# A four-layer gated transformer on one core: the head of layer 3's attention drawn into the 8-bit unit of layer 2, and gated adds moved from VectorE to ScalarE and GpSimd

## The chip, the cores and the metric

The kernel runs on one core of a Trainium2 chip. Its time is the device time of one execution in microseconds (us), of which the median over several runs is taken. The engines are TensorE (PE in the profile, with its weight loads as PEld), VectorE (DVE), ScalarE (ACT), GpSimd (POOL) and SyncE (SP, which issues transfers). The profile is one execution, recorded by the hardware.

## What is computed

The input x has 4 sequences of 256 tokens with 256 features. Four layers follow; each adds a cross attention and then a feed-forward unit, both on a layer norm of x and both gated:

```python
x = x + jnp.tanh(g_xattn[2]) * _L2_xattn_ref(_layernorm(x, axis=-1), ctx_512, ...)
x = x + jnp.tanh(g_ffn[2]) * _L2_ffn_ref(_layernorm(x, axis=-1), ...)
x = x + jnp.tanh(g_xattn[3]) * _L3_xattn_ref(_layernorm(x, axis=-1), ctx_512, ...)
x = x + jnp.tanh(g_ffn[3]) * _L3_ffn_ref(_layernorm(x, axis=-1), ...)
```

Layers 0 and 1 are of the same form with other units. What matters here are the units of layers 2 and 3. Their attention is plain: queries are x times a 256x256 matrix, keys and values come from a context of 64 positions, there are 16 heads of 16 features, the mask is causal, and the heads' outputs go through a 256x256 matrix. The feed-forward unit of layer 2 is a linear map in 8 bits: each row of the normalized x is scaled so that its largest magnitude is 127, rounded to whole numbers, multiplied with a weight rounded likewise, scaled back, and a bias is added. The feed-forward unit of layer 3 is a mixture of 8 experts, of which each token takes 2, and a shared expert.

## The kernel before

The 1024 tokens are 8 tiles of 128 tokens (tiles 0 to 7), and these make two groups of four (groups 0 and 1). x stays in SBUF for the whole kernel. The program is written with a tile framework: pools hand out buffers in turn, waits follow from who writes and reads a tile, and a scheduler of the framework, when the kernel is built, sets the order in which each engine's instructions stand in that engine's queue. So the order on an engine is not the order of the Python text. Each engine then works through its queue in order. `behind(later, sooner)` is the one means by which the text asks for an order within an engine.

**Attention of layers 2 and 3** (`attention23`, L1014). `queries(g)` makes the queries of one group: `layernorm` (L426: statistics on DVE L431 and L434, a square root on ACT L436, a reciprocal on DVE L439; then the normalization, on DVE L450 for layer 2, on ACT L447 for layer 3, where DVE first makes a shift, L443), `transposed` (PE L462, copies by ACT L169 and DVE L171), a product with the query weights (PE L477) and a scaling on ACT (L1034). Group 0's queries are made ahead of the loop over tiles, group 1's beside it.

`in_flight` (L514) runs the loop over tiles as a pipeline of depth three. In a step it makes the scores of one tile (PE L1058, causal mask L1048 for even tiles; maximum on DVE L1071, subtraction on DVE L1073, exponential on ACT L1082), weights the tile before (sum on DVE L491, reciprocal L492, product on POOL L493), attends with the tile before that (transposes on PE L507, two copies attnT on ACT L508, values on PE L1090, a copy ctxTok on ACT L1099, output weights on PE L1102), and adds the output of the oldest tile to x by `gated_add` (DVE L512, one instruction that reads the output from PSUM). ACT has one table of functions at a time; the square root and the exponential are in different ones, and each switch is an instruction ACT_TABLE_LOAD in its queue. Identity, copies and multiplications need no switch.

**The 8-bit unit** (`ffn2`, L1977). `rounded(g)` normalizes a group (L447), takes the largest magnitudes (DVE L1963), scales and rounds (DVE L1968, L1970), and adds the gated bias to x on POOL (L1974). `rounded(0)` is called near the end of layer 2's attention (`beside2`), `rounded(1)` when the loop of `ffn2` begins, since both groups stand in its list. For each group the loop then transposes (PE L1985, copy by ACT L1986), multiplies (PE L1991), scales (DVE L1995) and adds to x (POOL L1996).

**Buffers.** Transposed groups are in a pool xT of two buffers. Scores and their transposes (attn, attnT) take turns in a pool t4 of six buffers of 128x1024. Small row tiles (xn, y, ctxTok) take turns in a pool of seven.

## Time and profile before

| what | value |
|---|---|
| median of 3 runs | 839.23 us (837.9 to 839.84) |
| the profiled execution | 837.3 us, span 835.4 us |
| PE busy | 772.9 us, 93% of the span |
| DVE busy | 497.3 us, 60% |
| ACT busy | 291.6 us, 35% |
| POOL busy | 246.4 us, 29% |
| attention of layer 2 (first L477 to last L1102) | 539.76 to 592.25 us |
| attention of layer 3 (first L477 to last L1102) | 610.28 to 661.34 us |

The span runs from the first to the last instruction; the profiled execution's own time is longer by 1.9 us, for what lies around the span. A line of the timeline gives a start, a duration (of a merged run of instructions, where x4 or the like stands at its end), engine, line, operation, tiles and shapes; in brackets stand the idle time before it and what ended that. In the view by windows each row is a stretch of time with the busy time of each engine. The granted clock is the share of full speed that TensorE was given.

### The profile page before, as it was taken

What the parts mean: (1) busy time and instruction counts of PE and PEld (TensorE: products, weight loads), DVE (VectorE), ACT (ScalarE), POOL (GpSimd) and SP (SyncE); (2) the same over time, 40 slices, a digit from 0 to 9 for tenths busy, and PEclk for the clock granted to TensorE, in tenths of its full rate; (3) what the DMA queues carried; (4) which work ended last, traced back from release to release, by engine and by line L of the source; (5) the groups of instructions that cost most, each with busy time, mean ns of one, the idle gap of its engine ahead of it and who ended that gap; (6) DMA issues with size and microseconds to landing.
All of it is one profiled execution on the core that took longest, in us unless ns stands there. A gap on an engine that the chain in (4) does not pass through costs nothing.

```text
span 835.4 us, 12470 instructions
## 1 busy us (share of the span) xinstructions
PE 772.9 (93%) x4492; PEld 519.2 (62%) x4492; DVE 497.3 (60%) x1146; ACT 291.6 (35%) x508; POOL 246.4 (29%) x211
## 2 busy tenths in 40 slices
PE   6999999898999999999999989998579899999993
PEld 4544443687575776676555746655236557999993
DVE  5565454874682554545879559788869664334320
ACT  2121112343312333322633477166455521233320
POOL 1355454322132343321031200024424203344222
PEclk9999999999999999999999999899789999999997
DMA  9510215700121253324900001800000102222223
GB/s 343 189 39 0 62 40 204 262 22 4 29 72 40 72 141 83 74 35 123 378 17 7 1 1 37 324 24 1 26 0 2 51 8 78 55 51 46 33 26 71
DMA packets 32740, 64.14 MB, mean 77 GB/s; under 512 B 5121, under 2 KB 19713, under 8 KB 31905
## 3 DMA queue, kind: packets, MB, share of 16 engines
q1 hardware_dynamic: 25216, 52.56, 18.2%
q0 software_dynamic: 7104, 9.93, 7.3%
q8 instruction: 39, 0.64, 0.3%
q10 hardware_dynamic: 352, 0.79, 0.3%
q14 instruction: 29, 0.23, 0.1%
HBM read 53.86 MB, written 10.45 MB: 77 GB/s over the span
## 4 chain that ended last, share of the span: by engine, by line
PE 51%; DVE 9%; ACT 4%; issue 1%; POOL 1%; DMA 0%; POOLq 0%; DVEq 0%; ACTq 0%
PE wide L1435 9%; PE wide L477 7%; PE mm L1451 4%; PE mm L1525 3%; PE mm L709 3%; PE mm L1899 3%; PE mm L1883 2%; PE wide L961 2%; PE wide L1562 2%; PE wide L1563 2%; PE mm L1774 2%; PE mm L477 2%; DVE sm L491 1%; PE mm L507 1%; PE mm L1102 1%; PE wide L1058 1%
## 5 line engine op out<-in xcount | busy, mean ns | idle before, releaser
L493 POOL TENSOR_TENSOR attn<-attn,sm 128x1024 f32<-128x1024 f32 x32 | 61.1, 1913 | 229.3 <-DVE sm L492 179.0
L477 PE MATMUL wide<-xT,big 128*128 128x512 f32 (+1 forms) x240 | 108.6, 600 | 1.1 <-DVE shared L1656 0.9
L737 DVE TENSOR_TENSOR rope<-wide,big 128x512 f32<-128x512 f32 x96 | 59.6, 682 | 52.0 <-PE wide L477 52.0
L477 PEld LDWEIGHTS wide<-xT,big 128*128 128x128 f32 (+1 forms) x240 | 43.4, 188 | 57.3 <-issue 49.3
L1435 PE MATMUL wide<-blk,still 128*128 128x128 f32 x640 | 74.8, 275 | 0.6 <-DVE blk L1407 0.6
L1435 PEld LDWEIGHTS wide<-blk,still 128*128 128x128 f32 x640 | 73.1, 192 | 0.8 <-issue 0.8
L709 PE MATMUL mm<-vo,attnT 128*128 128x256 f32 x256 | 58.6, 382 | 1.5 <-ACT attnT L508 1.5
L477 PE MATMUL wide<-xT,dense 128*128 128x512 f32 (+1 forms) x120 | 55.1, 599 | 0.0
L709 PEld LDWEIGHTS mm<-vo,attnT 128*128 128x128 f32 x256 | 47.8, 190 | 11.4 <-ACT attnT L508 3.2
L508 ACT COPY attnT<-mm 128x512 f32<-128x512 f32 x64 | 34.4, 587 | 46.2 <-PE mm L507 45.7
L491 DVE TENSOR_REDUCE sm<-attn 128x16 f32<-128x1024 f32 x32 | 38.7, 1208 | 15.2 <-ACT attn L485 13.8
L1397 DVE COPY still<-big 128x1024 f32 x20 | 13.9, 693 | 52.0 <-PE wide L1435 44.5
L1466 POOL DMA_INDIRECT sums<-ring,scratch x20 | 31.6, 1578 | 40.4 <-ACT ring L1462 18.8
L1466 POOL DMA_INDIRECT sums<-ring,big x17 | 27.0, 1591 | 48.5 <-ACT ring L1545 18.2
L507 PE MATMUL mm<-ident,attn 128*128 128x128 f32 x256 | 33.7, 275 | 5.7 <-POOL attn L493 5.7
L1370 POOL DMA_INDIRECT xs<-xd,scratch x20 | 20.0, 1002 | 62.3 <-PE mm L1404 34.0
L512 DVE SCALAR_TENSOR_TENSOR x<-mm,tg,x 128x256 f32<-128x256 f32 x44 | 20.5, 471 | 29.4 <-PE mm L709 18.2
L1451 PE MATMUL mm<-big,hidden 128*128 x160 | 37.7, 379 | 0.0
L507 PEld LDWEIGHTS mm<-ident,attn 128*128 128x128 f32 x256 | 29.1, 141 | 13.3 <-POOL attn L493 8.5
L1443 ACT ACTIVATE hidden<-wide 128x512 f32<-128x512 f32 x20 | 12.0, 599 | 72.8 <-PE wide L1435 67.5
L477 PEld LDWEIGHTS wide<-xT,dense 128*128 128x128 f32 (+1 forms) x120 | 21.5, 185 | 24.4 <-issue 22.7
L791 ACT COPY big<-mm 128x512 f32<-128x512 f32 x16 | 8.6, 589 | 68.0 <-PE mm L779 61.7
(359 smaller groups left out, 1572.1 us busy)
## 6 DMA issues: line engine op xcount, KB each, us to landing
big<-in_L_w_gate_up SPq DMA_DIRECT2D x8, 1024.0 KB, 12.1
big<-in_L_w_down SPq DMA_DIRECT2D x8, 512.0 KB, 8.9
w_L_qk<-in_L_qk SPq DMA_DIRECT2D x4, 896.0 KB
big<-in_L_w SPq DMA_DIRECT2D x2, 1480.0 KB, 7.9
big<-in_L_w SPq DMA_DIRECT2D x2, 1110.0 KB
big<-in_L_wo SPq DMA_DIRECT2D x1, 2048.0 KB
big<-in_L_w SPq DMA_DIRECT2D x2, 1024.0 KB, 5.3
xd<-xn SPq DMA_DIRECT2D x16, 128.0 KB, 1.8
```

What stands on the lines that cost most here:

```text
L477: nc.tensor.matmul(ps, w(c), xT[:, c, :], start=(c == 0), stop=(c == 1))
L491: nc.vector.tensor_reduce(sm, e, AX.X, ALU.add)
L493: nc.gpsimd.tensor_tensor(e, e, sm.unsqueeze(2).to_broadcast([P, groups, n]), ALU.mult)
L507: nc.tensor.transpose(ps[:, i * P : (i + 1) * P], ev[:, pr * P : (pr + 1) * P], ident)
L508: nc.scalar.copy(aT[:, half * 4 : half * 4 + 4, :].rearrange("p i t -> p (i t)"), ps)
L709: nc.tensor.matmul(ps[:, :D], aT[:, s, :], vo[:, s, :], start=(s == 0), stop=(s == NP - 1))
L737: nc.vector.tensor_tensor(m[:, s, :].rearrange("q (b t) -> q b t", t=S), ps[:, s, :].rearrange("q (b t) -> q b t", t=S), table, ALU.mult,)
L1435: nc.tensor.matmul(ps[:, k, f : f + P], w[:, at : at + P], st[:, c * P : (c + 1) * P], start=(c == 0), stop=(c == 1),)
L1451: nc.tensor.matmul(ps[:, :D], hT[:, j * P : (j + 1) * P], self.w[:, bass.ds(r + j * D, D)], start=(j == 0), stop=(j == n - 1),)
L1466: nc.gpsimd.indirect_dma_start(out=self.sums[b % len(self.sums)], out_offset=bass.IndirectOffsetOnAxis(ap=self.scatter[:, b : b + 1].bitca ...
L1525: nc.tensor.matmul(ps[:n, f : f + P], w[:, c * FU0 + f : c * FU0 + f + n], st[:, c * P : (c + 1) * P], start=(c == 0), stop=(c == 1),)
L1899: nc.tensor.matmul(ps[:, :D], terms[:, k, f, i * P : (i + 1) * P], w2[:, f, :], start=(f == 0 and k == 0), stop=(f == 7 and k == 2),)
```

## The change

There are four parts.

- `layernorm` can load a table behind its square root. Group 1's norm in the attention of layers 2 and 3 loads that of the exponential there.
- In `in_flight`, tiles 0 to 5 no longer use `gated_add`. ACT multiplies the output with the gate into a tile y, and POOL adds y to x. Tiles 6 and 7 stay with DVE.
- In `ffn2`, layer 3's norm and queries for group 0 stand between group 0's 8-bit product and the call of `rounded(1)`; `attention23` of layer 3 takes them ready-made.
- The transposed whole numbers (xqT) and the normalized groups of layer 3 are in t4's buffers instead of those of xT and the row tiles.

```diff
-    def layernorm(g, scalar=False, after=()):
+    def layernorm(g, scalar=False, after=(), into=None, table=None):
...
+        if table is not None:
+            behind(nc.scalar.preload_act_table(table), made)
...
-            n = sb.tile([P, D], F32, tag="xn", name="xn", bufs=AHEAD + 2)
+            n = sb.tile([P, D], F32, tag="xn", name="xn", bufs=AHEAD + 2) if into is None else into[:, i, :]
...
-    def in_flight(scores, attend, gate, beside=iter(())):
+    def in_flight(scores, attend, gate, beside=iter(()), spared=0):
...
-                gated_add(i - 3, outs.pop(i - 3)[:, :D], gate)
+                t, ps = i - 3, outs.pop(i - 3)[:, :D]
+                if t < spared:
+                    y = sb.tile([P, D], F32, tag="xn", name="y", bufs=AHEAD + 2)
+                    nc.scalar.mul(y, ps, gate)
+                    nc.gpsimd.tensor_tensor(x[t], x[t], y, ALU.add)
+                else:
+                    gated_add(t, ps, gate)
...
+    def head_queries(layer, xT):
+        w_q = loaded[f"L{layer}"][:, :512].rearrange("p (c o) -> p c o", c=2)
+        pss = [ps_mm() for _ in range(2)]
+        for half, ps in enumerate(pss):
+            mm2(ps, lambda c: w_q[:, c, half * P : (half + 1) * P], xT)
+        for half, ps in enumerate(pss):
+            nc.scalar.mul(xT[:, half, :], ps, 0.25)
+        return xT
...
-            xn = layernorm(g, layer == 3)
+            if (layer, g) in kept:
+                qT.append(kept.pop((layer, g)))
+                return
+            into = t4([P, TPG, D], "normal") if layer == 3 else None
+            xn = layernorm(g, layer == 3, into=into, table=AF.Exp if g else None)
...
-        in_flight(scores, attend, gate, zip_longest(queries(1), beside))
+        in_flight(scores, attend, gate, zip_longest(queries(1), beside), NT - 2)
...
-        for g, (xq, xs) in enumerate([kept.pop("rounded"), rounded(1)]):
-            xqT = sb.tile([P, 2, TH], BF16, tag="xT", name="xT", bufs=2)
+
+        def unit(g, xq, xs):
+            xqT = t4([P, 1024], "xqT")[:, :TH].bitcast(BF16).rearrange("p (d t) -> p d t", d=2)
...
+        last = unit(0, *kept.pop("rounded"))
+        normal = t4([P, TPG, D], "normal")
+        kept[3, 0] = head_queries(3, transposed(layernorm(0, True, into=normal)))
+        unit(1, *rounded(1))
```

More of the change, by code (lines that the diff above doesn't have):

```diff
@@ L1019, in attention23 @@
         w = loaded[f"L{layer}"]
-        w_q = w[:, :512].rearrange("p (c o) -> p c o", c=2)
         w_o = w[:, 512:1024].rearrange("p (c o) -> p c o", c=2)
@@ L1029, in queries @@
             yield
-            pss = [ps_mm() for _ in range(2)]
-            for half, ps in enumerate(pss):
-                mm2(ps, lambda c: w_q[:, c, half * P : (half + 1) * P], xT)
-            for half, ps in enumerate(pss):
-                nc.scalar.mul(xT[:, half, :], ps, 0.25)
-            qT.append(xT)
+            qT.append(head_queries(layer, xT))
         for _ in queries(0):
@@ L1990, in ffn2 @@
                 for d in range(2):
-                    nc.tensor.matmul(
+                    made = nc.tensor.matmul(
                         ps[:, :D], xqT[:, d, i * P : (i + 1) * P], wqT[:, d, :], start=(d == 0), stop=(d == 1)
@@ L1996, in ffn2 @@
                 nc.gpsimd.tensor_tensor(x[t], x[t], y, ALU.add)
+            return made
+        last = unit(0, *kept.pop("rounded"))
+        normal = t4([P, TPG, D], "normal")
+        kept[3, 0] = head_queries(3, transposed(layernorm(0, True, into=normal)))
+        unit(1, *rounded(1))
     steps = [
```

## The prediction

> **What bounds the kernel now.** I read the busy shares, then the stretch in question (attention of layer 2, the 8-bit unit, attention of layer 3: 533 to 678 us) by windows, then the timelines of its engines. Outside it nothing changes, and after it the chain of waits is TensorE without gaps to 820, so what this stretch loses or wins the end loses or wins. Lines are those of the kernel before; tiles are counted 0 to 7, groups 0 and 1. The columns of the windows are: window, length, busy time of PE, PEld, DVE, ACT, POOL, granted clock, DMA share, GB/s.

> ```profile
> 560.00:578.00 18.00, 17.14 (x139) 10.31 (x137) 17.69 (x32) 11.22 (x23) 9.32 (x8) 1.00 0.00 1
> 578.00:592.00 14.00, 9.97 (x100) 6.73 (x97) 9.91 (x31) 9.09 (x18) 5.23 (x6) 1.00 0.00 0
> 592.00:607.00 15.00, 5.37 (x34) 2.66 (x31) 13.10 (x44) 4.72 (x11) 7.46 (x11) 0.65 0.11 37
> 607.00:626.00 19.00, 16.04 (x58) 7.72 (x58) 11.07 (x21) 11.18 (x18) 2.81 (x3) 0.83 0.00 0
> 644.00:661.00 17.00, 12.87 (x132) 8.59 (x125) 12.30 (x34) 9.88 (x18) 5.96 (x4) 1.00 0.05 17
> ```

> At 560 to 578 DVE is 98% and PE 95% busy: taking work from DVE alone leaves PE. At 592 to 607 PE has 5.4 us of work in 15, and its clock falls to 0.65: here is the gap that the change wants to fill. At 578 to 592 and 644 to 661 no engine is full, so a chain of latencies sets the pace. PE's timeline shows it:

> ```profile
> 579.07 1.13 PE L1102 MATMUL mm<-w_L,ctxTok 128*128 128x256 f32 x4 [0.49 <-ACT ctxTok L1099]
> 580.04 1.04 PE L507 MATMUL mm<-ident,attn 128*128 128x128 f32 x8
> 582.11 0.91 PE L1090 MATMUL mm<-attnT,values 128*32 128x128 f32 x16 [1.03 <-ACT attnT L508]
> 583.52 1.13 PE L1102 MATMUL mm<-w_L,ctxTok 128*128 128x256 f32 x4 [0.49 <-ACT ctxTok L1099]
> ...
> 601.33 0.70 PE L1985 MATMUL mm<-ident,xn 128*128 128x128 bf16 x4 [6.40 <-DVE xn L1970]
> ...
> 607.65 2.17 PE L462 MATMUL mm<-ident,xn 128*128 128x128 f32 x8 [2.33 <-ACT xn L447]
> 610.28 5.32 PE L477 MATMUL mm<-xT,w_L 128*128 128x512 f32 x8 [0.46 <-ACT xT L169]
> ```

> Each late tile goes PE, ACT, PE, ACT, PE: 3.7 us from one L1102 to the next (583.52, 587.22, 591.12). Whatever ACT does in between is on the path. The rows that price the parts, from ACT's and DVE's timelines:

> ```profile
> 549.16 1.28 ACT L1082 ACT_TABLE_LOAD   x1
> 550.46 1.06 ACT L1082 ACTIVATE attn<-attn 128x1024 f32<-128x1024 f32 x1
> ...
> 618.22 1.28 ACT L1082 ACT_TABLE_LOAD   x1
> 620.09 1.06 ACT L1082 ACTIVATE attn<-attn 128x1024 f32<-128x1024 f32 x1 [0.58 <-DVE attn L1073]
> ...
> 652.77 1.28 ACT L436 ACT_TABLE_LOAD   x1
> ```
> ```profile
> 582.11 1.80 DVE L443 SCALAR_TENSOR_TENSOR shift<-mv,rstd 128x4 f32<-128x4 f32 x1
> ...
> 599.09 1.45 DVE L1968 TENSOR_SCALAR xn<-xn,xi 128x256 f32<-128x256 f32 x2
> 600.47 1.01 DVE L1970 TENSOR_SCALAR xn<-xn 128x256 bf16<-128x256 f32 x2
> 601.39 0.60 DVE L1968 TENSOR_SCALAR xn<-xn,xi 128x256 f32<-128x256 f32 x2
> ```

> Engines run their queues in order, so I took the order in which the changed kernel stands on each engine and set these durations along it, each start being the later of its engine and its inputs.

> **Step A, attention of layer 2.** The exp table now loads behind the second square root (539.9), where ACT idles 3.8 us before L1034: free there. The first exponential starts at 549.15 instead of 550.46, 1.3 us gained. Little of it arrives: ACT's new order puts both L1034 ahead of exponential 1, and DVE's puts sum 0 ahead of subtraction 1, which ends at 552.65 instead of 551.4; sum 1 then waits for exponential 1 (552.7 to 553.75). L507 of tile 0 starts at 554.9 instead of 555.18: 0.3 gained.

> [...]

> Six gated adds (L512) leave DVE: start to start with the next operation 0.39 us each (571.40 to 571.79), 2.3 us. ACT gets six multiplications from PSUM; the trace has none. Its bounds are the 128x256 copy from PSUM (L1099, 0.37) and the activation with pointers (L447, 0.59); I take 0.37, the same source. POOL gets six adds at 0.70 (L1996, four in 2.77) between products of 1.90 (L493).

> What this adds is a wait. Statistics of tile 2 (L431) now wait for POOL's add, which stands behind the product of tile 5. By the walk DVE reaches them at 572.95; the product runs 571.9 to 573.8, the add ends at 574.55. Behind them wait subtraction 6 and sum 6, and on ACT exponential 6 stands ahead of the copies of tile 4: exponential 6 at 576.25, attnT of tile 4 at 578.1 (before 577.03), then exponential 7, the sqrt table and multiplication 4: attnT of tile 5 at 583.05 (before 581.50). Later multiplications fit beside L507. The last L1102 starts at 592.8 (before 591.12), L447 of the rounding at 588.7 (before 587.07). **A: +1.6 us**; between -1.3 (no stall, table gain kept) and +2.8 (each multiplication at 0.59: 6 x 0.2 more).

> **Step B, 8-bit unit to the first output of attention 3.** Rounding of group 0 keeps its pace: its L1991 at 595.4. New: its four y (L1995, 1.66) run at 596 to 597.6, POOL's adds end at 599.3, statistics, root and shift at 601.7, normalization (4 in 2.08), L462, L477. As before, L477 starts 3.28 us after the normalization starts (610.28 - 607.00): 605.0, and takes 5.3 at the low clock, since PE was idle before: 610.3. Scores of tile 0 come at about 611.3 (before 615.53): 4.2 us ahead.

> But group 1's rounding has moved behind all this: its L447 stands on ACT behind group 0's normalization and one xT copy and starts at 605.0 (before 594.86); maxima and rounding end at 610.2, transposes behind L477, L1991 at 612.4 (before 603.43), y at 613.5 to 615.1, adds to 616.9. DVE's queue has the maximum of tile 0, then y, the statistics of group 1, the maximum of tile 1 (1.2), the shift, and only then subtraction 0: at 619.45 (before 618.77). ACT has root, exp table (1.28, on the path again), normalization of group 1 (2.08), then exponential 0: 622.5 (before 620.09). Sums 0 and 1 both precede reciprocal 0: 626.4 (before 623.66). PE idles from 614.6 to 621.0, so L462, L1058 and part of L477 of group 1 run at half clock, to 629.7; L1090 of tile 0 at 631.85 (before 628.96), +2.9. **B: +1.3**; bounds -1.0 (full clock) and +2.7 (POOL's bias adds over the rounding: 1.45 - 0.60 + 1.01 - 0.48, 1.4 us).

> The rows for that: shift took 1.80 us while POOL's product ran (581.99 to 583.89), otherwise 0.14 to 0.16. [...]

> The reductions (1.21 beside a product as elsewhere) show no such loss, so I count none for attention.

> **Step C, attention of layer 3.** DVE is relieved, but its queue waits in turn for exponentials; the tail from tile 2 on is again 3.7 us per tile. L1102 of tile 2 starts at 644.25 (before 641.50). One thing is added: the sqrt table now stands ahead of ctxTok of tile 5 instead of behind it: 1.28 + 0.30, some 1.0 on the path. Last L1102 at 663.85 (before 660.21). **C: +0.7**, between -0.3 and +1.1.

> Free: xqT and the normalized group use the pool of six 128x1024 buffers, whose earlier tenants (attn and attnT of layer 2) are read by 592; would they not be, PE would wait. SP's queue is the same.

> Sum: 1.6 + 1.3 + 0.7 = +3.6. The profiled execution took 837.3 us (span 835.4): 840.9. The median shown, 839.23, is 1.9 above it, so 842.8 as a median.

> **Rivals.**
> 1. *Early queries carry* (faster). For it: scores of tile 0 are ready 4 us early. If group 1 ended before the first maximum (613.5), subtraction 0 would follow it and not 619.45: 6 us less, 836.8. It decides from 3.6 us on, subtraction 0 at 615.8. Against it: DVE's queue order. 9%.
> 2. *POOL's adds come in time* (no change). With tile 2 updated before 573 and the sqrt load hidden, A and C fall by 2.4: 840.4. For it: the stall is 1.6 us and hangs on one product. 17%.
> 3. *Lock-out* (slower still): rounding of group 1 and shifts collide with POOL, +2: 844.8. Against it: bias adds end at 608.4, the rounding starts at 608.1. 12%.
> Forecast, 842.8: 62%.

> Faster by over 0.2% (1.7 us, about what a measurement here tells from no change): 9%, within 17%, slower 74%. The range is 838.0 to 846.8. Above it takes in all upper ends together (2.8 + 2.7 + 1.1 = 6.6, 845.8) and 1.0 for the spread of the runs. Below, the lower ends together (-2.6, 836.6) need every unknown at its best and go with rival 1: what lies under 838.0 is left out, under 2 in 10.

> **What would show it.** A: statistics of tile 2 waiting for POOL, attnT of tile 5 past 582.5. B: scores of tile 0 near 611 but exponential 0 past 621; PE idle some 6 us after group 1's L1991. C: a table load just before ctxTok of tile 5. I am wrong if exponential 0 comes before 619, or attention 2 ends before 591.

## The result, and the profile after

The changed kernel takes 848.76 us as a median of 4 runs (845.83 to 850.68), the kernel before 838.88 us on the same chip (4 runs, 837.9 to 839.84). The ratio is 1.0118, with a 95% interval of 1.0091 to 1.0145: slower by 9.9 us. The forecast was slower by 3.6. The direction was right; the size was not, and the time lies 2 us above the range.

The line numbers have moved: L1102 of the kernel before is L1117 in the changed one, L507 is L509, L1090 is L1105, L508 is L510, L1099 is L1114, L1082 is L1097, L462 is L464, L477 is L479, L1048 is L1063, L1073 is L1088, L493 is L495, L447 is L449. New are the multiplication L527, the add L528 and the early table load L440.

The first thing to do with two traces is to cut them where the prediction cut them. Executions differ by some us in when layer 2's attention begins (537.8 to 544.7 us over all profiled runs of this study, with no edit ahead of it), so I compare lengths of stages, and whole times only by medians:

| stage | before | after | difference | predicted |
|---|---|---|---|---|
| A: first queries of attention 2 to its last output product | 51.36 | 56.52 | +5.2 | +1.6 (-1.3 to +2.8) |
| B: from there to the first values product of attention 3 | 37.84 | 39.70 | +1.9 | +1.3 (-1.0 to +2.7) |
| C: from there to the last output product of attention 3 | 31.25 | 33.54 | +2.3 | +0.7 (-0.3 to +1.1) |
| the rest: from there to the end of the span | 175.19 | 176.24 | +1.1 | 0 |

The sum is +10.4, close to the 9.9 of the medians. (The two spans themselves, 835.4 and 848.7 us, differ by 2.9 us more; that part lies ahead of A.) B is inside its bounds. A is 2.4 us outside, C 1.2, and the rest was not priced at all. TensorE's timeline of the changed kernel has all three misses:

```profile
579.38 0.59 PE L1063 MATMUL wide<-causal,ident 128*128 128x512 bf16 x1 [1.72 <-DVE attn L1088]
579.76 1.91 PE L1117 MATMUL mm<-w_L,ctxTok 128*128 128x256 f32 x4
...
582.75 1.97 PE L509 MATMUL mm<-ident,attn 128*128 128x128 f32 x8
...
590.11 0.91 PE L1105 MATMUL mm<-attnT,values 128*32 128x128 f32 x16 [1.40 <-ACT attnT L510]
...
608.77 2.16 PE L464 MATMUL mm<-ident,normal 128*128 128x128 f32 x8 [5.73 <-ACT normal L449]
...
627.90 2.16 PE L464 MATMUL mm<-ident,normal 128*128 128x128 f32 x8 [6.47 <-ACT normal L449]
...
663.84 1.36 PE L1117 MATMUL mm<-w_L,ctxTok 128*128 128x256 f32 x4 [1.44 <-ACT ctxTok L1114]
665.00 1.91 PE L509 MATMUL mm<-ident,attn 128*128 128x128 f32 x8
...
681.65 9.67 PE L479 MATMUL wide<-xT,w_L_sgu 128*128 128x512 f32 x18
```

Look at the durations beside the waits. L1117 takes 1.13 us and L509 1.04 to 1.09 at full clock; behind the wait of 1.72 they take 1.91 and 1.97. Behind the 1.44, L1117 takes 1.36 and L509 1.91. The windows of the same trace say why (columns as in the prediction; the granted clock is the number ahead of the last two):

```profile
580.00:585.00 5.00, 5.00 (x15) 2.97 (x14) 3.12 (x6) 2.30 (x6) 2.50 (x2) 0.50 0.02 3
...
665.00:670.00 5.00, 4.35 (x32) 3.01 (x31) 0.69 (x3) 2.02 (x4) 0.73 (x1) 0.70 0.00 0
```

At 580 to 585 TensorE is busy all the time, at a granted clock of 0.50. In the kernel before, this stretch ran at 1.00. There the same mask stands in the same place, ahead of the output product of tile 3, and doesn't wait:

```profile
574.04 0.60 PE L1048 MATMUL wide<-causal,ident 128*128 128x512 bf16 x2
574.60 1.13 PE L1102 MATMUL mm<-w_L,ctxTok 128*128 128x256 f32 x4
```

What sets the wait of A off is what the prediction named. VectorE's timeline, and below it GpSimd's:

```profile
577.71 0.43 DVE L431 BATCH_NORM_STATS2 st<-x 128x6 f32<-128x256 f32 x1 [1.64 <-POOL x L528]
578.05 1.27 DVE L1088 TENSOR_TENSOR attn<-wide,mx 128x512 f32<-128x512 f32 x2
```
```profile
575.08 1.91 POOL L495 TENSOR_TENSOR attn<-attn,sm 128x1024 f32<-128x1024 f32 x1 [0.90 <-DVE sm L494]
576.95 0.73 POOL L528 TENSOR_TENSOR x<-x,y 128x256 f32<-128x256 f32 x1
```

The statistics of tile 2 wait 1.64 us for GpSimd's add, which stands behind a product of 1.91. Counted from the stage's start they begin at 35.0 us; the walk had put them at 34.8 (574.55 less 539.76). The subtraction behind them ends at 579.32, and there the walk went blind: it followed that subtraction to its exponential on ScalarE, and did not ask who else waits for it on TensorE. Up to there it is right (exponential 6 starts 36.7 us after the stage's start, 36.5 walked); the copies attnT of tile 4, which wait for TensorE, start at 41.3 instead of the 38.3 walked.

ScalarE's timeline of the changed kernel, for B and C:

```profile
625.95 1.28 ACT L440 ACT_TABLE_LOAD   x1
627.25 2.08 ACT L449 ACTIVATE normal<-x,shift,rstd 128x256 f32<-128x256 f32 x4
629.23 1.04 ACT L1097 ACTIVATE attn<-attn 128x1024 f32<-128x1024 f32 x1
...
661.94 1.28 ACT L436 ACT_TABLE_LOAD   x1
...
663.44 0.35 ACT L1114 COPY ctxTok<-mm 128x256 f32<-128x256 f32 x1
```

The exponential table is on the path of exponential 0 (between root and normalization of group 1), and the sqrt table stands just ahead of ctxTok of tile 5, both as walked. Exponential 0 starts 30.0 us after the last output product of attention 2 (29.7 walked, 29.0 before).

### The profile page after: what moved, and what is told of

It reads as the page before. It is cut to its first block, busy times and chain, and to the rows that moved or that the text cites. A ratio compares the mean times of both kernels' runs of the same rounds, so it can differ in the third digit from the quotient of the medians.

```text
span 848.7 us, 12478 instructions
## 1 busy us (share of the span) xinstructions
PE 781.5 (92%) x4492; PEld 524.9 (62%) x4492; DVE 493.8 (58%) x1134; ACT 297.2 (35%) x520; POOL 255.3 (30%) x223
## 5 line engine op out<-in xcount | busy, mean ns | idle before, releaser
L495 POOL TENSOR_TENSOR attn<-attn,sm 128x1024 f32<-128x1024 f32 x32 | 61.2, 1913 | 215.7 <-DVE sm L494 190.8
L479 PE MATMUL wide<-xT,big 128*128 128x512 f32 (+1 forms) x240 | 108.9, 601 | 1.1 <-DVE shared L1671 0.9
L479 PEld LDWEIGHTS wide<-xT,big 128*128 128x128 f32 (+1 forms) x240 | 43.7, 189 | 57.5 <-issue 49.5
L479 PE MATMUL wide<-xT,dense 128*128 128x512 f32 (+1 forms) x120 | 55.1, 598 | 0.0
L493 DVE TENSOR_REDUCE sm<-attn 128x16 f32<-128x1024 f32 x32 | 38.9, 1218 | 23.5 <-ACT attn L487 13.8
L510 ACT COPY attnT<-mm 128x512 f32<-128x512 f32 x64 | 34.7, 588 | 42.0 <-PE mm L509 41.7
L509 PE MATMUL mm<-ident,attn 128*128 128x128 f32 x256 | 36.3, 288 | 3.5 <-POOL attn L495 3.5
L509 PEld LDWEIGHTS mm<-ident,attn 128*128 128x128 f32 x256 | 31.4, 149 | 11.7 <-POOL attn L495 5.6
L479 PEld LDWEIGHTS wide<-xT,dense 128*128 128x128 f32 (+1 forms) x120 | 21.5, 185 | 24.4 <-issue 22.1
L753 POOL TENSOR_TENSOR rotated<-rope 128x512 f32<-128x512 f32 x12 | 15.3, 1274 | 59.4 <-DVE rope L745 59.4
L431 DVE BATCH_NORM_STATS2 st<-x 128x6 f32<-128x256 f32 x64 | 26.0, 414 | 11.7 <-POOL x L528 5.4
```

The source lines that it names most:

```text
L431: made = nc.vector.bn_stats(st, x[g * TPG + i])
L479: nc.tensor.matmul(ps, w(c), xT[:, c, :], start=(c == 0), stop=(c == 1))
L493: nc.vector.tensor_reduce(sm, e, AX.X, ALU.add)
L495: nc.gpsimd.tensor_tensor(e, e, sm.unsqueeze(2).to_broadcast([P, groups, n]), ALU.mult)
L509: nc.tensor.transpose(ps[:, i * P : (i + 1) * P], ev[:, pr * P : (pr + 1) * P], ident)
L510: nc.scalar.copy(aT[:, half * 4 : half * 4 + 4, :].rearrange("p i t -> p (i t)"), ps)
```

## The experiments

My theory after the result: the mechanisms of the prediction are there, but each wait of 1.4 to 1.7 us that they put into TensorE's chain of late tiles is paid twice, once as the wait and once as some us of half clock behind it. The rivals were that the parts of the change cost by something else (VectorE's work taking longer beside GpSimd's, the extra work on ScalarE), and that early queries would pay if group 1 were not in their way. Times are medians; ratios are to the kernel before, run on the same chip, with 95% intervals. Stage lengths are of one profiled execution. Two of the expectations (52.5 and 57.7 us for attention 2) count to the end of the last output product; the table and the results count to its start (51.36 and 56.52).

**The gated adds alone.** The kernel before with the spared adds and nothing else.

```diff
...
-        in_flight(scores, attend, gate, zip_longest(queries(1), beside))
+        in_flight(scores, attend, gate, zip_longest(queries(1), beside), NT - 2)
```

> The kernel before with only the spared gated adds (six per layer by ScalarE and GpSimd). Theory (the spared adds make the loss in attention 2: statistics of tile 2 wait for GpSimd's add, behind them subtraction 6, and for that TensorE's mask of layer 3's first tile, after which the clock falls): attention 2 from its first L477 to its last L1102 takes 4 to 6 us longer than the 52.5 of before, a dip of the granted clock stands near tile 3, attention 3 is 1 to 2.5 longer since the sqrt table stands ahead of a ctxTok copy here too; in all 844 to 847. Rival 1 (the early exp table and the order that it brings make the loss): within 1 us of before. Rival 2 (most of the loss is the stretch ahead of attention 2, which no edit touches): within 2 us of before once that stretch is left out.

Measured: 844.55 us, ratio 1.0066 (1.0043 to 1.009); A is 56.78 us. The whole loss of A comes with the adds. For attention 3 the expectation was wrong: B and C together are 0.8 us shorter than before (36.35 and 31.99). The sqrt table does stand ahead of a ctxTok here, and TensorE waits 1.44 us for it (657.14), but the granted clock stays at 1.00 from 645 to 665 us, and C is only 0.7 us longer.

**The early table alone**, in both layers.

```diff
...
-            xn = layernorm(g, layer == 3)
+            xn = layernorm(g, layer == 3, table=AF.Exp if g else None)
```

> The kernel before with only the early load of the exponential's table. Theory: attention 2 gains 0.3 us at the first L507 and keeps it or loses up to 0.5; in layer 3 the load is hidden behind the normalization, worth up to 1.3, against which a sqrt table ahead of a ctxTok copy costs about 1; in all 837.5 to 840. Rival 1 (the table's new order makes the loss): attention 2 is 3 to 5 us longer, 842 to 844.

Measured: 841.79 us, ratio 1.0039 (1.0018 to 1.006); A 51.25, B 39.02, C 32.14. The time is over the theory's range, and A is not what the rival said either. By the ratio the loads cost 3.3 us, all of it behind attention 2. TensorE's timeline of this kernel shows one place:

```profile
613.22 6.56 PE L479 MATMUL mm<-xT,w_L 128*128 128x512 f32 x8 [1.39 <-ACT xT L169]
```

In layer 3 the scheduler put the load ahead of group 0's copy xT: the first queries wait 1.39 us (0.46 before) and take 6.56 us (5.32 before). Ahead of a ctxTok the sqrt table makes TensorE wait 1.44 us here too (660.57), again at a granted clock of 1.00.

**The early table in layer 2 only.**

```diff
...
-            xn = layernorm(g, layer == 3)
+            xn = layernorm(g, layer == 3, table=AF.Exp if g and layer == 2 else None)
```

> The kernel before with the early exp table in layer 2 alone. Theory (the load in layer 2 lies in idle time of ScalarE, the loss of the run with both tables was layer 3's, where the load stands ahead of an xT copy and of ctxTok): attention 2 within 0.3 of 51.3 us, the rest as before, 837.5 to 838.7 in all, no difference. Rival (the first exponential, 1.3 us earlier, carries): attention 2 at 50.3 or less, 836.5 to 837.5.

Measured: 837.74 us, ratio 1.0005 (0.9987 to 1.0024); A 51.45, B 37.87, C 31.34. No difference. The first exponential does start 1.3 us earlier (9.4 us after the stage's start, 10.7 before), and none of it arrives at the end of the stage.

**The early queries alone.** The changed kernel with VectorE's adds and without early tables.

```diff
-        in_flight(scores, attend, gate, zip_longest(queries(1), beside), NT - 2)
+        in_flight(scores, attend, gate, zip_longest(queries(1), beside))
...
-            xn = layernorm(g, layer == 3, into=into, table=AF.Exp if g else None)
+            xn = layernorm(g, layer == 3, into=into)
```

> The kernel before with only group 0's norm and queries of layer 3 ahead of group 1's rounding (and the buffers that go with it). Theory: attention 2 is as before within 0.5; the scores of tile 0 of layer 3 come some 3 us earlier against the rounding's normalization than before, but subtraction 0 stands behind group 1's statistics on VectorE, so the first L1090 of attention 3 comes 1 to 2.5 us later than before, against the normalization of the rounding; in all 840 to 843. What the edit would give if early queries carried: 4 us less, 835.

Measured: 842.10 us, ratio 1.0043 (1.0026 to 1.0061): a loss. The profiled execution was the longest of its runs (848.04), so I draw nothing from its stages.

**The changed kernel without the spared adds**, to see whether the parts add up.

```diff
-        in_flight(scores, attend, gate, zip_longest(queries(1), beside), NT - 2)
+        in_flight(scores, attend, gate, zip_longest(queries(1), beside))
```

> The changed kernel with all gated adds back on VectorE (early queries and both early tables stay). Theory (the parts add up: spared adds +5.7 alone, early queries and tables +4 each alone, but these two share what is late in layer 3): attention 2 back at 51.0-51.6 us, 842 to 844.5 in all, some 4 to 6.5 under the changed kernel. Rival (the parts hide one another, so taking one away gives nothing): 846 or more.

Measured: 843.05 us, ratio 1.0063 (1.0027 to 1.0098); A 51.44, B 38.39, C 34.00. Taking the adds away gives A back in full. The rest of the change keeps a loss in C as large as the changed kernel's: TensorE waits 2.02 us for a ctxTok at 648.49 (the L1117 and the L509 behind it take 1.13 and 1.04, as at full clock), and behind a wait of 1.03 at 655.23 an L1117 at 656.64 takes 1.93 and an L509 at 658.36 1.92. The three parts alone cost 0.66, 0.39 and 0.43%, together 1.48, the whole change 1.18%. They may share some of their price, but the intervals (0.2 to 0.3 to either side of each) don't show it.

**Statistics later.** The changed kernel, where the statistics of the rounding's first group stand behind the last subtraction, and its root behind the last exponential, so that no subtraction is queued behind a wait for GpSimd.

```diff
...
-        xn = layernorm(g, True)
+        xn = layernorm(g, True, after=() if g else (kept["apart"], kept["raised"]))
```

> The changed kernel, with the statistics of the first group's rounding placed on VectorE behind the last subtraction of layer 2's attention (an order within one engine; nothing else). Theory: no wait for GpSimd ahead of subtraction 6, no dip of the clock; attention 2 falls from 57.7 us to 53.5 to 55, the whole to 844 to 846. Rival 1 (the early table's order): attention 2 stays within 1 us of 57.7, the whole at 847.5 to 850.

Measured: 844.29 us, ratio 1.0074 (1.0049 to 1.0099). The wait for GpSimd ahead of subtraction 6 is gone and the whole is inside the theory's range, but A is still 54.80 (55.9 as the expectation counts it, where it said 53.5 to 55): multiplication 4, load and root now stand ahead of attnT of tile 5, TensorE waits 1.77 us for it, and the clock at 585 to 590 us is 0.66. One late wait has taken the place of the other.

**Only four tiles spared, statistics later.** No multiplication ahead of the sqrt table.

```diff
...
-        in_flight(scores, attend, gate, zip_longest(queries(1), beside), NT - 2)
+        in_flight(scores, attend, gate, zip_longest(queries(1), beside), TPG)
```

> The changed kernel with the rounding's first statistics behind the last subtraction and exponential, and only tiles 0 to 3 of each attention with their adds on ScalarE and GpSimd. So on ScalarE no multiplication stands ahead of the sqrt table, and in attention 2 the load stands ahead of ctxTok of tile 5, not of attnT of tile 5. Theory (in the run with the later statistics, what was left of the loss in attention 2 was multiplication 4, load and root ahead of attnT of tile 5, with the half clock behind that wait): attention 2 falls from 54.8 us to 51.5-53, attention 3 from 34.0 to 32-33, 839.5 to 842 in all. Rival (the multiplications themselves, 0.47 us each in ScalarE's chain of the first four tiles, cost it): attention 2 stays over 54, 843.5 or more.

Measured: 843.70 us, ratio 1.0066 (1.0044 to 1.0089); A 52.96 as the theory had it, but C 33.19, and the whole 1.7 us over the theory's range and inside the rival's, whose A (over 54) it doesn't have. In A the clock stays at 1.00 and the load costs a wait of 1.44 ahead of an L1117. In C a wait of only 1.03 (655.66) is followed by an L509 of 1.91, 1.04 at full clock: half clock again.

**The mask later.** This is the run for the step that I had missed. TensorE's queue of the changed kernel has the causal mask of attention 3's first tile (L1063) ahead of L1117 of tile 3 of attention 2; it needs the wide buffer that the late subtraction frees. Here it stands behind the last L1117.

```diff
...
+                    if layer == 3 and t == 0:
+                        behind(mask, kept["out2"])
...
```

> The changed kernel, with one edit: the causal mask matmul of attention 3's first tile, which stood on TensorE ahead of L1117 of tile 3 of attention 2, now stands behind the last L1117 of attention 2. Theory (of the loss in attention 2 that the prediction missed, some 3.5 us, this matmul's wait for the wide buffer, 1.7 us, and the half clock behind it are the cause): attention 2 falls from 56.5 us to 53-54.5, 845 to 847 in all. Rival (ScalarE's chain sets the pace there, with multiplication, table load and root ahead of attnT of tile 5): attention 2 stays at 55.5 or more, 848 to 850.

Measured: 846.21 us, ratio 1.0088 (1.007 to 1.0106); A falls from 56.52 to 53.23, while B (39.67) and C (33.54) stay. TensorE's timeline and windows of this kernel:

```profile
580.16 1.13 PE L1119 MATMUL mm<-w_L,ctxTok 128*128 128x256 f32 x4 [0.49 <-ACT ctxTok L1116]
...
583.92 0.92 PE L1107 MATMUL mm<-attnT,values 128*32 128x128 f32 x16 [0.98 <-ACT attnT L510]
...
588.78 0.92 PE L1107 MATMUL mm<-attnT,values 128*32 128x128 f32 x16 [1.40 <-ACT attnT L510]
```
```profile
580.00:585.00 5.00, 3.63 (x30) 2.14 (x30) 3.91 (x9) 3.05 (x8) 0.72 (x1) 1.00 0.01 3
```

L1119 here is the L1117 of the changed kernel: it waits 0.49 and takes 1.13. One mask, two matmuls that together take 0.6 us where they don't wait, was worth 3.3 us in a place where it had to wait. What is left of A's loss, 1.9 us, is what the prediction had walked (1.6), and its steps are met too: attnT of tile 4 starts 38.6 us after the stage's start (38.3 walked), attnT of tile 5 43.5 (43.3 walked). The interval of the whole overlaps with that of the changed kernel, so it is the stage that shows this, not the total.

**The root later.** The same question for C: the sqrt table behind ctxTok of tile 5, as in the kernel before.

```diff
...
+        if root is not None:
+            behind(made, root)
...
```

> The changed kernel with one edit: in attention 3 the square root of the next layer norm, and with it the sqrt table, stands on ScalarE behind ctxTok of tile 5 (as in the kernel before) and not ahead of it. Theory (of step C the load and root ahead of that copy, 1.6 us, make TensorE wait 1.4 us, and the half clock behind it doubles the price): attention 3 falls from 33.5 us to 31.5-32.5, no half clock in it after the granted clock of 0.7 at 665 us; 846.5 to 848 in all. Rival (the multiplication that now stands between root and attnT of tile 6 gives the wait back there): attention 3 stays over 33, 848 to 850.

Measured: 844.93 us, ratio 1.0094 (1.0061 to 1.0127); C falls from 33.54 to 31.63, the rest from 176.24 to 175.14, A (56.35) and B (39.61) stay. TensorE's timeline of this kernel:

```profile
658.25 1.13 PE L1121 MATMUL mm<-w_L,ctxTok 128*128 128x256 f32 x4 [0.55 <-ACT ctxTok L1116]
659.22 1.04 PE L511 MATMUL mm<-ident,attn 128*128 128x128 f32 x8
660.70 0.91 PE L1107 MATMUL mm<-attnT,values 128*32 128x128 f32 x16 [0.44 <-ACT attnT L512]
```

From 640 us on, no wait over 0.6, no long row, and the granted clock is 1.00 from 640 to 675 us. The whole is 1.6 us under the theory's range, but its interval is wide. So C's excess hangs on this one load. That the rest's does is not shown. The row of 9.67 at 681.65 us in the changed kernel, about 0.9 us longer than the two rows and the wait that stand there before, is half clock again (granted 0.67 at 680 to 685 us); but the early table alone has such a row (9.67 at 673.47) with no half clock in C, and the changed kernel without the spared adds has half clock in C and no such row. And in the eight kernels without that row the rest varies from 175.1 to 176.1 us by itself.

**Group 1's product further back.** The kernel before with early queries, and group 1's 8-bit product behind the scores of tile 0, so that subtraction 0 is ahead of it on VectorE. It tests what the first rival of the prediction lives on.

```diff
-        unit(1, *rounded(1))
+        kept["unit1"] = unit, rounded(1)
...
+            if "unit1" in kept:
+                yield
+                made, rest = kept.pop("unit1")
+                made(1, *rest)
...
```

> The kernel before with the early queries alone, and with group 1's 8-bit product moved further back, into attention 3's loop behind the scores of tile 0; no spared adds, no early table. So subtraction 0 stands on DVE ahead of group 1's four y. Theory (it was group 1's place on DVE's and ACT's queues that ate the 4 us which the scores of tile 0 win): from the last L1102 of attention 2 to the first L1090 of attention 3 falls from 37.8 us to 32-34; tiles 4 and later then wait for group 1, two more table loads (1.28 each) come in, so C grows by 1 to 4; 835 to 839 in all. Rival (the early scores have no use, since something else holds exponential 0): that stretch stays over 36.5, and with the two loads the whole takes 841 or more.

Measured: 848.38 us, ratio 1.0117 (1.0099 to 1.0135); A 51.28, B 36.98, C 40.68. The theory fails. The rival's numbers hold, its reason doesn't. TensorE's timeline, then ScalarE's:

```profile
640.47 3.60 PE L479 MATMUL mm<-xT,w_L 128*128 128x512 f32 x8
```
```profile
615.89 1.06 ACT L1102 ACTIVATE attn<-attn 128x1024 f32<-128x1024 f32 x1
```

Exponential 0 (L1102 in this kernel's numbering) comes 7.4 us earlier than before, counted from the start of attention 2 (73.0 against 80.3), as hoped. But B is only 0.9 us shorter. The copies attnT of tile 0 stand on ScalarE behind group 1's root and normalization, two table loads and exponential 2, and start at 630.57, so the first values product waits:

```profile
631.19 1.15 PE L1110 MATMUL mm<-attnT,values 128*32 128x128 f32 x16 [2.77 <-ACT attnT L510]
```

And group 1's queries (L479 at 640.47) come 18 us later (97.5 against 79.3), so tiles 4 to 7 wait, and C grows by 9.4. In both placings of group 1 that were run, its work passes the same queues as tile 0's, and what one gains the other loses.

**A warm clock.** The kernel before with matmuls that nobody reads (10 behind group 0's 8-bit product, 6 behind group 1's), to price the half clock by itself. The causal mask of attention 3's first tile and a few of VectorE's statistics change places with them.

```diff
+            warm = ps_wide()
+            for i in range(10 if g == 0 else 6):
+                nc.tensor.matmul(warm[:, i % 2, :], xqT[:, 0, :P], xqT[:, 1, :], start=True, stop=True)
```

> The kernel before, with matmuls that nobody reads (128x512 in bf16, ten behind group 0's 8-bit product, six behind group 1's) in TensorE's idle time of 596 to 607 us; the causal mask of attention 3's first tile stands behind them. Theory (the idle time there costs by the half clock in which L462 and L477 then run): granted clock over 0.9 at 600 to 610 us, first L477 of attention 3 under 3.5 us (5.3 before), the stretch from attention 2 to the first L1090 of attention 3 falls from 37.8 us to 34-36, 834.5 to 837 in all. Rival (the latencies of the other engines cover it, or the granted clock doesn't follow): that stretch within 0.7 of 37.8, 838 to 839.

Measured: 836.54 us, ratio 0.9978 (0.9961 to 0.9995); B 35.89. Stretch and time are as the theory had them, but the granted clock at 600 to 610 us is only 0.68 and 0.63, and the first L477 takes 3.70 us. Then with **26 and 12**, and VectorE's queue as in the kernel before:

> The kernel before with more unread matmuls in TensorE's idle time between the groups of the 8-bit product: 26 behind group 0, 12 behind group 1 (10 and 6 in the run before, where the granted clock was still 0.68 and 0.63 at 600 to 610 us). Theory (half clock in the gap costs what the first queries of attention 3 take longer): granted clock at 600 to 610 us over 0.9, first L477 of attention 3 under 3 us, the stretch from attention 2 to the first L1090 of attention 3 at 34.5-35.5 us; 835 to 836.5 in all. Rival (what the ten and six gained is all there is, as exponential 0 waits for the other engines): that stretch stays within 0.5 of 35.9 us, 836 to 837.5.

Measured: 836.08 us, ratio 0.997 (0.995 to 0.999); A 51.31, B 35.61, C 30.81. TensorE's timeline and windows of this kernel:

```profile
612.70 3.70 PE L477 MATMUL mm<-xT,w_L 128*128 128x512 f32 x8 [0.56 <-ACT xT L169]
...
619.81 3.70 PE L477 MATMUL mm<-xT,w_L 128*128 128x512 f32 x8
```
```profile
600.00:605.00 5.00, 3.69 (x21) 1.63 (x19) 5.00 (x15) 0.05 (x1) 3.34 (x5) 1.00 0.00 0
605.00:610.00 5.00, 4.51 (x19) 2.23 (x18) 4.38 (x18) 2.17 (x5) 2.71 (x4) 0.66 0.01 3
```

The granted clock is 1.00 at 600 to 605 but 0.66 at 605 to 610, not over 0.9. The first queries take 3.70 us, as long as the second group's at full clock: my "under 3" was wrong, 3.70 is all there is, and the shorter filling had it already. So the rival was right on the second step (35.61 against 35.89: nothing more to gain), and the theory on the first: work of no use, put where TensorE idles, makes the kernel faster by about 0.3%, and the two versions with it are the only ones here that beat both kernels. B is 2.2 us shorter; 1.6 of it is the row of the first queries, which took 5.32 us before.

## Why the prediction was wrong

- **A, +1.6 predicted, +5.2 measured.** Confirmed: the statistics of tile 2 wait for GpSimd, to 0.2 us where walked; the early table gains nothing (the run with it in layer 2 alone); attnT of tile 5 comes late. The step that failed is "behind them wait subtraction 6 and sum 6, and on ACT exponential 6": subtraction 6 also frees the wide buffer in which the mask of layer 3's first tile is written, and that mask stands on TensorE ahead of the output product of tile 3. With it moved, A is +1.9. It was worth 3.3 us: the wait, and the half clock (the runs don't part the two).
- **Multiplications** took 0.47 us each, between my bounds, 0.10 over the value I took. At most 0.6 in all, and the run with the mask moved leaves only 0.3 of A unexplained.
- **B, +1.3 predicted, +1.9 measured: right.** Scores of tile 0 come from group 0's early queries, subtraction 0 waits behind group 1's y and statistics, TensorE idles 6.47 us (6.4 walked) before group 1's L464, which takes 2.16 at half clock (granted 0.50 at 625 to 630 us).
- **C, +0.7 predicted, +2.3 measured.** The mechanism was named, the size was not: 1.0 for the load on the path, while the run with the root behind ctxTok gives back 1.9. The term that was too small is the load's: I counted its wait and not the half clock behind it. The kernel with the spared adds alone has the same wait of 1.44 at full clock, and its C is +0.7: the wait by itself is about what was walked.
- **The rest, 0 predicted, +1.1 measured.** The term was put at nothing because "outside it nothing changes" and TensorE was read as "without gaps to 820". The trace before has a wait of 0.50 at 674.44 there, and the changed kernel has half clock (granted 0.67 at 680 to 685). What sets that off stays open, and part of the 1.1 can be the spread between executions.
- **Rival 1, early queries carry:** wrong, and not only for its condition. Even with subtraction 0 in front, the gain of 7.4 us on exponential 0 is down to 0.9 at the first values product, and tiles 4 to 7 lose 9.4.
- **Rival 2, adds in time:** the run with the statistics moved has no such wait, and is still slower by 0.74%; in A, load, root and multiplication then stand in the chain. The rival's other condition, a hidden sqrt load, it doesn't meet.
- **Rival 3, lock-out, +2:** no run shows the +2. In the attention VectorE's sums take 1.22 us beside GpSimd's new adds, 1.21 before. In group 1's rounding the first two scalings (614.28), beside the last bias add, take 0.82 together, the next two 0.61. One shift takes 1.77 beside GpSimd's product (589.47), as one of the kernel before took 1.80.
- **The table load** takes what its row says: the load at 625.95 takes 1.28 us and the normalization starts 0.02 us behind it, as the exponential does behind the load at 549.16 in the kernel before.

One bookkeeping error runs through A and C. The prediction read the low clock in the long gap of the kernel before (592 to 607) and priced it in B, the step that came out right. It did not ask of each new wait in A and C whether half clock would follow. The trace before had a warning, half clock behind a short wait (granted clock 0.50 at 628 to 630):

```profile
626.04 1.09 PE L507 MATMUL mm<-ident,attn 128*128 128x128 f32 x8 [1.84 <-POOL attn L493]
627.07 1.97 PE L1058 MATMUL wide<-kbd,xT 64*128 64x256 f32 x8
```

So my theory after the result holds for the waits that the changed kernel has ahead of its long rows, not for each wait of this length. What stays open is what exactly tips the clock; the waits listed below show that length alone doesn't. No run has both the mask and the root moved, so that the two repairs add up is not shown either.

## What to carry to other kernels

When a walk along the queues delays an instruction, list everyone who waits for it, on every engine, buffers included: the matmul that costs may be one for the next stage that a scheduler put ahead of this one's. Price a new wait in a chain of TensorE's latencies at its length, put about as much again into the upper bound for half clock behind it (an estimate from two repairs: the mask moved, which had waited 1.72 us, gave 3.3 us, the load moved, behind which TensorE had waited 1.44, gave 1.9; half clock came behind some waits and not behind others), and read the granted clock window by window before and after. An early start of the first tile was worth nothing here, where its later steps and the later tiles stood behind other work in in-order queues.

## What the runs showed of the hardware that I had not expected

Behind the gaps of 5.73 and 6.47 us of the changed kernel (608.77 and 627.90) L464 takes 2.16 us, and 1.04 at full clock (673.42). Why waits of like length end differently no run here tests, nor whether the idle time summed over some us decides.

The loss in A is as steady as its cause. Three kernels that share the mask's wait have A at 56.5, 56.8 and 56.4 us; with VectorE's adds seven profiled executions, the one before among them, have it at 51.3 to 51.5, and one, the long one of the early queries alone, at 53.1.
